# An adaLN block on one core: a new order of the opening steps, and the late modulation weights loaded in quarters

## Chip, cores and metric

The kernel runs on one core of a Trainium2 chip (trn2). The metric is device time in microseconds (us) of one launch. "KB" is 1024 bytes.

## The reference, cut to what matters

The input `x` has 2 x 4096 tokens of width 512. A conditioning vector `c` (2 x 512) gives six modulation rows per batch:

```python
mod = (_silu(L0_c) @ L0_wmod).reshape(2, 6, 1, -1)          # wmod: 512 x (6*512), float32
sa, ca, ga, sb, cb, gb = (mod[:, n] for n in range(6))
ga, gb = signed_floor(ga), signed_floor(gb)                   # magnitude at least 0.25
h = _layernorm(x) * (1 + ca) + sa
x = x + ga * attn(h)      # rms norm with gamma, h @ W_qkva.T (512 -> 3*512), y = scan(sigmoid(a), kv), q*y
h = _layernorm(x) * (1 + cb) + sb
x = x + gb * ffn(h)       # gate, up (512 -> 1408), silu(gate)*up, down (1408 -> 512)
```

All inputs and weights of `ffn` are quantized to a 4-bit grid in blocks of 16 along the contracted axis. `attn` runs along the tokens: `y` at a token is `a` times `y` of the token before plus `kv`. The modulation rows are numbered 0 to 5 here, in the order `sa, ca, ga, sb, cb, gb`.

## The kernel before, in words

The attention half works on 16 blocks of 512 tokens. A block has four tiles of 128 tokens and, for the projections, four groups of 128 output channels. One pair (block, group) is a slot; slots are numbered block after block, four to a block, so slot 4 is the first of the second block. In a slot `mix` (L414 on, the matmul at L430) makes the three projections of one group: 3 parts of 12 matmuls of 128 x 512, in hi and lo halves of float16. Slots 0 to 3 are the opening, written out as one list of words, `OPENING` (L698); slots from 4 on come from the loop at L847.

Every engine executes its instructions in the order in which the program names them (L846, a manual schedule), and so does the sync engine (SP), which issues nearly all DMAs: a word further left in `OPENING`, or a call further up in the loop, is earlier in the queue of its engine. The words that matter here, with a tile number g or with a group e and a piece k behind them:

- Loads, all on SP: `xl_g` a tile of x (L360, 256 KB); `wl e_h` half of a group of W_qkva (L292, 384 KB); `wm s_k` one quarter (128 of 512 rows, 256 KB) of the weights of modulation row s (`load_mod`, L223). `c` and `gT` are small.
- Modulation of the first batch: `ms s_k` multiplies one quarter of wmod with the conditioning vector on TensorE (PE, L230), spread over all partitions; `ca` (L790) and `sa` (L791) copy rows 1 and 0 out of PSUM. `rows` (L244) makes rows 0, 1, 2 for both batches, `rst` and `rdm` copy and send them, `rtr`, `gqa`, `gqf` turn and floor row 2.
- A tile's layer norm: `mo`, `ag` statistics (L154, L159, VectorE = DVE), `rs` (L164, GpSimd = POOL), `ce` (L170) and `sh` (L176) on DVE, `xq` square (L385, ScalarE = ACT), `xg` on POOL (L390, L392), `xh` the hi half on ACT (L398), `xo` the lo half on DVE (L403), and `xt` the DMA transpose of both halves on SP (`norm_turn`, L409).
- A group's weights: `sq` (ACT, L295), `sum` (PE, L300), `cl`, `pw`, `dg`, `sp` (PE, L329), `sc` (DVE, L334), `hi` (ACT, L343), `lo` (DVE, L348).
- `mm e_q`: group 0 of the first block is done in four quarters of 128 tokens, 36 matmuls of 128 x 128 each, so that `mm0_q` needs only the transpose of tile q. For groups 1 to 3, q is one of the three parts, over all 512 tokens.
- After that, `ga`, `sn`, `cy`, `ro`, `yh`, `yt`, `jo`, `re`, `od`: gate, scan, read-out, a second DMA transpose (`yt`, L471), residual, store.

In the loop a slot issues on SP, in this order: two weight tiles of the feed-forward half (256 KB each, only to find their block maxima), a tile of x for seven tiles later (256 KB), the transpose `xT` of the tile four ahead, the transpose `yt`, and last any modulation load. Four `xT` tiles must have landed before the first slot of the next block can begin. There is one `yh` buffer.

The weights of modulation rows 3, 4 and 5, needed only in the feed-forward half, are loaded in the loop. With `MODS = 10` (L844) a whole one (1024 KB) is loaded at the end of slots 5, 6 and 7; the 24 matmuls of `mod_rows(3, 4, 5)` (L244) follow in slot 10, and the rows are stored in slot 11. Slot 5 also loads two rows for the second batch (L283, 256 KB each). The rows 3 and 4 are read back first in slot 36.

```python
            if MODS - 5 <= slot < MODS - 2:
                load_mod(slot - MODS + 8)
```

The feed-forward half then runs over 64 tiles of 128 tokens, 72 matmuls for gate and up (L946) and 33 for down (L993) per tile.

Of the kernel before, what the change touches and what calls it, by code (L numbers as in the profile page):

```python
# [20 lines left out]
KC = D // P  # L21
# [23 lines left out]
def tile_adaln_block(  # L45
# [24 lines left out]
    def ctile(shape, dtype, name, tag=None):  # L70
        return const.tile(shape, dtype, name=name, tag=tag or name)
# [60 lines left out]
    def run(steps):  # L132
        for _ in steps:
            pass
# [53 lines left out]
    def atile(shape, dtype, name, bufs=1):  # L188
        return apool.tile(shape, dtype, name=name, tag=name, bufs=bufs)
# [23 lines left out]
    gT = atile([P, KC], F32, "gT")  # L213
# [9 lines left out]
    def load_mod(s, k0=0, k1=KC):  # L223
        S.dma_start(
            wm[s][:, k0:k1, :],
            wmod[k0 * P : k1 * P, s * D : (s + 1) * D].rearrange("(k p) e -> p k e", p=P),
        )
# [126 lines left out]
    def norm_load(g):  # L354
        i, t = divmod(g, KC)
        if i not in xrows:
            xrows[i] = apool.tile([P, KC, D], F32, name="xr", tag="xr", bufs=4)
        xld[g] = xrows[i][:, t, :]
        b, t0 = divmod(g * P, N)
        S.dma_start(xld[g], x[b, t0 : t0 + P, :])  # L360

    def norm_moments(g):
        xstat[g] = moments(xld[g])
# [51 lines left out]
    def new_xT():  # L415
        return apool.tile([P, 2 * KC, TB], F16, name="xT", tag="xT", bufs=2)
# [4 lines left out]
    def mix(i, xT, e, got):  # L421
        ps = [bank(3 * (e % 2) + j) for j in range(3)]
        got.append((i, e, ps))
        width = P if i == 0 and e == 0 else TB
        for t in range(0, TB, width):
            for pp, part in zip(ps, PARTS):
                n = 0
                for k in range(KC):
                    for wp, xp in PASSES:
                        T.matmul(  # L430
                            pp[:, t : t + width],
                            wqT[e][:, wp, k, part, :],
                            xT[:, xp * KC + k, t : t + width],
                            start=n == 0,
                            stop=n == 3 * KC - 1,
                        )
                        n += 1
                yield

    def gates(i, e, ps):  # L440
        sig = apool.tile([P, TB], F32, name="sig", tag="sig", bufs=1)
        A.activation(sig, ps[0], AF.Sigmoid, scale=us[:, e, 2:3])
        return i, e, ps, sig
# [137 lines left out]
    rows = [(i, col, w, ams) for i in range(IC) for col, w, ams in ((0, w_gate, am_g), (1, w_up, am_u))]  # L581
# [13 lines left out]
    def load_units(items):  # L595
        got = []
        for kind, arg in items:
            if kind in ("max", "rows"):
                got.append((kind, arg, load_rows(arg[2], arg[0])))
            elif kind in ("maxd", "down"):  # L600
                got.append((kind, arg, load_down(*arg)))
            else:
                got.append((kind, arg, None))
        return got
# [84 lines left out]
    ca = [ctile([P, D], F32, "ca0", tag="mod_c0"), None]  # L689
    sa = [ctile([P, D], F32, "sa0", tag="mod_s0"), None]  # L690
# [5 lines left out]


    OPENING = """  # L698
    warm0 wl0_1 gT wl0_0 c xl_0 xl_1 wm1_0 xl_2 sq0_2 wm1_1 sq0_3 wm1_2 xl_3 sq0_1 wm1_3
    sq0_0 wm0_0 mo_0 sg sum0 wm0_1 mu wm0_2 cl0 ag_0 pw0 mo_1 wm0_3 ms1_0 wl1_0 ag_1 dg0  # L700
    wl1_1 rc0 mo_2 xl_7 rs_0 sp0 wm2_0 ag_2 ms1_1 sc0_0 wm2_1 rs_2 wm2_2 sc0_1 ms1_2 wm2_3
    sc0_3 hi0_0 xl_10 rs_1 mo_3 xl_9 ms1_3 wl2_0 sc0_2 xl_4 ag_3 lo0_0 ms0_0 rs_3 ca hi0_1
    ce_2 ms0_1 ce_0 ms0_2 ce_1 ms0_3 warm1 ce_3 sq1_0 lo0_2 sa sq1_1 sh_0 sq1_2 sh_2 xq_0
    sh_1 sq1_3 xg_0 mo_7 xq_1 sum1 sh_3 xh_0 xg_1 cl1 ag_7 xq_2 xo_0 rows pw1 xh_1 ce_7 xt_0
    xg_2 xq_3 rc1 mo_9 xl_6 dg1 xh_2 xo_1 wl2_1 sq2_1 ag_9 xt_1 xo_2 rs_9 sq2_0 sp1 mm0_0
    mo_4 rst2 xg_3 xt_2 rst0 sc1_0 rst1 ag_4 rdm0 sc1_2 wl3_1 xh_3 rtr rs_7 sc1_1 xl_8 xo_3
    mm0_1 gqa rdm1 hi1_0 sc1_3 xt_3 rs_4 sh_7 sq2_2 mo_6 xl_5 xq_7 mm0_2 wl3_0 gqf hi1_1
    xg_7 ag_6 sq2_3 pg_0 rs_6 lo1_2 xh_7 mm0_3 ce_4 lo1_0 sum2 ga_0 pg_1 mm1_0 cl2 sq3_2
    mo_5 pw2 sq3_0 sh_4 sq3_1 dg2 ag_5 xq_4 sn_0 sp2 sq3_3 xg_4 mm1_1 sc2_0 cy_0 sc2_1 rs_5
    xh_4 sc2_2 hi2_0 sc2_3 sum3 ro_0 hi2_1 mm1_2 cl3 lo2_0 yh_0 pw3 lo2_2 dg3 ga_1 yt_0 rc3  # L710
    sn_1 mm2_0 ce_6 cy_1 ro_1 jo_0 sh_6 sp3 mm2_1 yh_1 re_0 sc3_2 sc3_1 xq_6 yt_1 sc3_3 od_0
    sc3_0 hi3_1 xg_6 ce_5 mm2_2 hi3_0 lo3_2 xh_6 lo3_0 xo_4 mm3_0 sh_5 xt_4 pg_3 xq_5 xo_6
    xg_5 rc2 xt_6 xo_7 mm3_1 ga_2 mo_8 xh_5 xt_7 xo_5 sn_2 xt_5 mm3_2 pg_2 cy_2 ag_8 ro_2
    rs_8 ce_8 yh_2 sh_8 yt_2 xq_8 xg_8
    """

    def opening(xT, nxT):
# [118 lines left out]
    def step(gen, n=1):  # L836
        for _ in range(n):
            if gen is not None:
                next(gen, None)

    units, coming = [], []
    rows = None
    NS = NBLK * KC
    MODS = 10  # L844
    plan = [[]] * (KC + 1) + plan
    order = tc.manual_schedule(engines={V.engine, A.engine, G.engine, S.engine, T.engine})  # L846
    with order:  # L847
        xT, nxT = new_xT(), new_xT()
        gate, joining = opening(xT, nxT)
        for slot in range(KC, NS + 3):  # L850
            i, e = divmod(slot, KC)
            if e == 0 and slot < NS:
                xT = nxT
                nxT = new_xT() if i + 1 < NBLK else None
            units, coming = coming, load_units(plan[slot]) if slot < len(plan) else []
            g = slot + KC
            if g + 3 < NT:
                norm_load(g + 3)
            cur = None
            if slot < NS:  # L860
                got = []
                step(mix(i, xT, e, got), 3)
                cur = got[0]
            late = rows
            rows = mod_rows(3, 4, 5) if slot == MODS else None
            if slot == KC:
                gate = gates(*gate)
            if len(joining) == 2 or slot >= NS + 2:
                store(*residual(*joined(*joining.pop(0))))
            if g < NT:  # L870
                norm_hi(g)
            if gate is not None:
                gate = scan(*gate)
                carry_on(*gate)
            if g + 2 < NT:
                norm_moments(g + 2)
            if gate is not None:
                gate = read_out(*gate)
            if g < NT:
                norm_lo(g, nxT)  # L880
            if gate is not None:
                joining.append(turned(*halves(*gate)))
            if g + 2 < NT:
                norm_stats(g + 2)
            for u in units:
                u.advance(1)
            if g + 1 < NT:
                norm_center(g + 1)
            for u in units:
                u.advance(2)  # L890
                u.advance(3)
            if cur is not None:
                cur = gates(*cur)
            if g + 1 < NT:
                norm_shift(g + 1)
                norm_square(g + 1)
            for u in units:
                u.advance(4)
            coming = [Unit(*c_) for c_ in coming]
            for u in coming:  # L900
                u.advance(0)
            if g + 1 < NT:
                norm_gain(g + 1, G)
            for u in units:
                u.advance(5)
                u.advance(6)
            assert all(u.step == 7 for u in units)
            if MODS - 5 <= slot < MODS - 2:
                load_mod(slot - MODS + 8)
            if late is not None:  # L910
                mod_store(*late)
            if slot == KC + 1:
                ca[1] = mod_load(1, 1, "mod_c1")
                sa[1] = mod_load(0, 1, "mod_s1")
            if slot == NS // 2 + KC:
                mods_for(0)
            if slot == NS // 2 + KC + 2:
                gbs[0] = mod_load(5, 0, "mod_gb")
            if slot in (NS - 6, NS - 5):
                for n in range(2):  # L920
                    n += 2 * (slot - NS + 6)
                    x1s[n] = load_x1(n)
            if NS - 5 <= slot < NS - 1:
                n = slot - NS + 5
                xst[n] = stats_x(x1s[n])
                if n in (1, 2):
                    run(quant_x(n - 1, x1s.pop(n - 1), xst.pop(n - 1)))
            gate = cur
# [192 lines left out]
```

## Time and profile before

| | |
|---|---|
| median of 3 runs | 1911.56 us (1910.95 to 1913.81) |
| profiled execution, own time | 1914.65 us |
| its span, first to last instruction | 1912.9 us |
| PE busy | 1895.3 us, 99% |
| DVE, ACT, POOL busy | 84%, 52%, 21% |
| granted TensorE clock, mean | 0.998 of full |

The span is cut into stages as follows, by when the matmuls start: the opening up to 63.2 us, attention from there to 538.8 us, the feed-forward half up to the end. Reading: a row of the windows view gives a stretch, its length, busy time with number of instructions for PE, PEld (weight loads, which overlap PE), DVE, ACT and POOL, then the granted TensorE clock, the mean busy share of the 16 DMA engines (it can pass 1 where transfers overlap), and GB/s. A row of the chain of waits is start, duration, what; "DMA xT<-hl" there is the time from the issue of a transpose to its landing. In the timeline, SPq is the issue of a DMA, and its duration is that of the issue alone.

### The profile page before, as it was taken

What the parts mean: (1) busy time and instruction counts of PE and PEld (TensorE: products, weight loads), DVE (VectorE), ACT (ScalarE), POOL (GpSimd) and SP (SyncE); (2) the same over time, 40 slices, a digit from 0 to 9 for tenths busy, and PEclk for the clock granted to TensorE, in tenths of its full rate; (3) what the DMA queues carried; (4) which work ended last, traced back from release to release, by engine and by line L of the source; (5) the groups of instructions that cost most, each with busy time, mean ns of one, the idle gap of its engine ahead of it and who ended that gap; (6) DMA issues with size and microseconds to landing.
All of it is one profiled execution on the core that took longest, in us unless ns stands there. A gap on an engine that the chain in (4) does not pass through costs nothing.

```text
span 1912.9 us, 25829 instructions
## 1 busy us (share of the span) xinstructions
PE 1895.3 (99%) x9342; PEld 902.5 (47%) x9342; DVE 1601.9 (84%) x2670; ACT 998.2 (52%) x1702; POOL 409.6 (21%) x596
## 2 busy tenths in 40 slices
PE   8999999999999999999999999999999999999998
PEld 5444444444444444444444444444444444444444
DVE  7878899999869988888888888878888888888865
ACT  5555577777755444444444444445444544444432
POOL 5545566666420100100000000000000001000000
PEclk9999999999999999999999999999999999999999
DMA  7787789988733533443344333433344334433433
GB/s 219 208 213 196 170 201 201 213 201 198 152 82 69 88 72 64 79 77 67 64 73 80 70 64 79 80 71 72 64 82 77 64 64 79 80 64 64 68 64 58
DMA packets 469040, 203.26 MB, mean 106 GB/s; under 512 B 426102, under 2 KB 427382, under 8 KB 468912
## 3 DMA queue, kind: packets, MB, share of 16 engines
q1 hardware_dynamic: 454464, 168.09, 41.3%
q0 software_dynamic: 14448, 33.52, 9.0%
q8 instruction: 73, 1.20, 0.3%
q14 instruction: 55, 0.45, 0.1%
HBM read 62.86 MB, written 33.58 MB: 50 GB/s over the span
## 4 chain that ended last, share of the span: by engine, by line
PE 95%; DMA 2%; DVE 2%; issue 0%; ACT 0%; SPq 0%; POOL 0%; DVEq 0%; ACTq 0%
PE mm L946 47%; PE sd L993 24%; PE mm L430 23%; DMA xT<-hl 1%; DMA xr<-in_L_attn_x_dram 1%; DMA yt<-yh 1%; PE sd L230 0%; DVE ld L176 0%; PE sd L244 0%; DVE hl L403 0%; DVE xn L107 0%; DVE hid L966 0%; ACT row L267 0%; DVE hhl L126 0%; DVE amh L148 0%
## 5 line engine op out<-in xcount | busy, mean ns | idle before, releaser
L946 PEld LDWEIGHTS <-x2T 128*128 128x128 f16 x4608 | 450.9, 98 | 469.0 <-issue 0.9
L430 PE MATMUL mm<-xT,wqT 128*128 128x512 f16 (+1 forms) x2412 | 501.0, 370 | 7.0 <-DMA xT<-hl 6.9
L946 PE MATMUL mm<-wuT,x2T 128*128 128x512 f16 (+1 forms) x2304 | 487.7, 361 | 0.6 <-DVE hid L966 0.6
L946 PE MATMUL mm<-wgT,x2T 128*128 128x512 f16 (+1 forms) x2304 | 487.7, 361 | 0.0
L993 PE MATMUL sd<-wdT,hT 128*128 128x512 f16 x2112 | 465.8, 379 | 0.0
L430 PEld LDWEIGHTS <-wqT 128*128 128x128 f16 x2412 | 230.1, 98 | 278.0 <-issue 9.8
L993 PEld LDWEIGHTS <-hT 128*128 128x128 f16 x2112 | 206.7, 98 | 242.7
L961 ACT ACTIVATE silu<-mm,u 128x512 f32<-128x512 f32 (+1 forms) x192 | 124.6, 650 | 285.5 <-PE mm L946 281.8
L966 DVE SCALAR_TENSOR_TENSOR hid<-mm,u,silu 128x512 f32<-128x512 f32 (+1 forms) x192 | 128.5, 673 | 138.4 <-PE mm L946 129.9
L635 POOL TENSOR_SCALAR rstd<-vs 128x1 f32<-128x1 f32 x64 | 14.5, 227 | 989.8 <-ACT sq L633 989.8
L144 ACT ACTIVATE u<-ud,rms 128x1 f32<-128x1 f32 x64 | 18.9, 295 | 278.4 <-DVE rms L140 278.4
L121 ACT ACTIVATE sle<-sl 128x512 f16<-128x512 f32 (+2 forms) x162 | 146.9, 907 | 0.0
L114 ACT ACTIVATE she<-sh 128x1408 bf16<-128x1408 bf16 (+1 forms) x128 | 128.3, 1002 | 4.2
L466 ACT COPY yh<-y 128x1024 uint16<-128x1024 uint16 x64 | 66.9, 1045 | 91.8 <-DVE y L459 76.8
L1017 POOL DMA_DIRECT2D out_dram<-o x63 | 55.5, 881 | 271.0 <-DVE o L1011 267.2
L123 DVE SCALAR_TENSOR_TENSOR xn<-hid,xn 128x1408 f32<-128x1408 f32 x64 | 103.6, 1619 | 3.7 <-ACT hid L117 3.7
L107 DVE TENSOR_TENSOR xn<-hid,inv 128x1408 f32<-128x1408 f32 x64 | 104.0, 1625 | 2.2
L126 DVE SCALAR_TENSOR_TENSOR hhl<-hid,xn 128x1408 f16<-128x1408 f32 x64 | 104.0, 1625 | 2.2
L148 DVE TENSOR_REDUCE amh<-hid 128x88 f32<-128x1408 f32 x64 | 103.7, 1620 | 2.2
L117 ACT ACTIVATE hid<-xn 128x1408 f32<-128x1408 f32 x64 | 88.1, 1377 | 30.9 <-DVE xn L107 30.9
L123 DVE SCALAR_TENSOR_TENSOR xn<-ld,xn 128x512 f32<-128x512 f32 (+1 forms) x98 | 67.0, 684 | 29.0 <-ACT ld L117 28.8
L485 POOL TENSOR_TENSOR xr<-xr,y 128x512 f32<-128x512 f32 x64 | 81.6, 1276 | 19.5 <-ACT y L477 16.0
(129 smaller groups left out, 1913.3 us busy)
## 6 DMA issues: line engine op xcount, KB each, us to landing
ld<-out_dram SPq DMA_DIRECT2D x65, 256.0 KB, 2.9
xr<-in_L_attn_x_dram SPq DMA_DIRECT2D x64, 256.0 KB, 3.5
out_dram<-xr POOLq DMA_DIRECT2D x64, 256.0 KB, 3.9
out_dram<-o POOLq DMA_DIRECT2D x63, 256.0 KB, 3.9
ld<-in_L_ffn_w_gate_dram SPq DMA_DIRECT2D x22, 256.0 KB, 3.2
ld<-in_L_ffn_w_up_dram SPq DMA_DIRECT2D x22, 256.0 KB, 3.3
ld<-in_L_ffn_w_down_dram SPq DMA_DIRECT2D x16, 256.0 KB, 3.3
scratch<-in_L_attn_W_qkva_dram SPq DMA_DIRECT2D x8, 384.0 KB, 5.0
```

Of the source, the lines that this page charges most:

```text
L107: V.tensor_tensor(blocks(xn), blocks(src), spread(inv, nb), ALU.mult)
L114: A.activation(blocks(she), spread(sh, nb), AF.Copy, scale=WPEAK)
L117: A.activation(a, xn, AF.Abs, scale=MAGIC)
L121: A.activation(blocks(sle), spread(sl, nb), AF.Copy, scale=WPEAK)
L123: V.scalar_tensor_tensor(out=xn, in0=a, scalar=FLOOR, in1=xn, op0=ALU.max, op1=ALU.add)
L126: V.scalar_tensor_tensor(out=nq, in0=a, scalar=FLOOR, in1=xn, op0=ALU.max, op1=ALU.subtract)
L148: V.tensor_reduce(am, src.rearrange("p (b k) -> p b k", k=QB), AX.X, ALU.max, apply_absolute_value=True)
L430: T.matmul(pp[:, t : t + width], wqT[e][:, wp, k, part, :], xT[:, xp * KC + k, t : t + width], start=n == 0, stop=n == 3 * KC - 1,)
L946: T.matmul(pp[:, : n1 - n0], x2T[:, xp * KC + k, :], wt[:, wp * KC + k, n0:n1], start=n == 0, stop=n == 3 * KC - 1,)
L961: A.activation(sl[:, :w], pairs[j][0][:, :w], AF.Silu, scale=u[:, 0:1])
L966: V.scalar_tensor_tensor(out=hid[:, n0:n1], in0=pairs[j][1][:, : n1 - n0], scalar=u[:, 1:2], in1=sl[:, : n1 - n0], op0=ALU.mult, op1=ALU.mult,
L993: T.matmul(pd, hT[:, hp * IC + k, :], wdT[:, wd_chunk(wp, k), :], start=n == 0, stop=n == 3 * IC - 1,)
```

## The change

Two things. The word list `OPENING` is a new one: the four transposes of the first block, in the new order 0, 3, 1, 2, are consecutive in SP's queue, where the list before had two loads between the first and the second and two between the third and the fourth. The eleven x tiles, the weight halves and the modulation quarters are the same, in another order; so are the compute words of all engines. And rows 3 to 5 of the modulation weights are loaded in twelve quarters, one at the end of each of the slots 5 to 16, with the matmuls in slot 19 and the stores in slot 20.

SP's queue around the first transposes, by words:

```
before: ... wl1_0 wl1_1 xl_7 wm2_0 wm2_1 wm2_2 wm2_3 xl_10 xl_9 wl2_0 xl_4
        xt_0 xl_6 wl2_1 xt_1 xt_2 wl3_1 xl_8 xt_3 xl_5 wl3_0
after:  ... wl1_1 wl1_0 wm2_3 xl_5 wm2_2 wm2_0 wm2_1 xl_4 wl2_1 wl2_0
        xt_0 xt_3 xt_1 xt_2 xl_10 xl_9 xl_7 xl_6 wl3_1 wl3_0 xl_8
```

The diff, its long lists cut to the parts spoken of:

```diff
-    warm0 wl0_1 gT wl0_0 c xl_0 xl_1 wm1_0 xl_2 sq0_2 wm1_1 sq0_3 wm1_2 xl_3 sq0_1 wm1_3
-    sq0_0 wm0_0 mo_0 sg sum0 wm0_1 mu wm0_2 cl0 ag_0 pw0 mo_1 wm0_3 ms1_0 wl1_0 ag_1 dg0
...
-    sh_1 sq1_3 xg_0 mo_7 xq_1 sum1 sh_3 xh_0 xg_1 cl1 ag_7 xq_2 xo_0 rows pw1 xh_1 ce_7 xt_0
-    xg_2 xq_3 rc1 mo_9 xl_6 dg1 xh_2 xo_1 wl2_1 sq2_1 ag_9 xt_1 xo_2 rs_9 sq2_0 sp1 mm0_0
-    mo_4 rst2 xg_3 xt_2 rst0 sc1_0 rst1 ag_4 rdm0 sc1_2 wl3_1 xh_3 rtr rs_7 sc1_1 xl_8 xo_3
-    mm0_1 gqa rdm1 hi1_0 sc1_3 xt_3 rs_4 sh_7 sq2_2 mo_6 xl_5 xq_7 mm0_2 wl3_0 gqf hi1_1
-    xg_7 ag_6 sq2_3 pg_0 rs_6 lo1_2 xh_7 mm0_3 ce_4 lo1_0 sum2 ga_0 pg_1 mm1_0 cl2 sq3_2
...
+    warm0 wl0_0 gT wl0_1 c xl_3 xl_1 xl_0 wm1_0 sq0_0 xl_2 sq0_1 wm1_1 wm1_2 sg sq0_3 wm0_0
+    mu wm1_3 sq0_2 mo_3 wm0_1 sum0 ag_3 wm0_2 cl0 mo_1 wm0_3 pw0 wl1_1 ag_1 wl1_0 mo_0 dg0
...
+    ca ce_1 ms0_2 ce_2 ms0_3 warm1 ce_0 sq1_2 ce_3 sa sq1_3 sh_0 sq1_1 sh_3 xq_0 sh_1 sq1_0
+    xg_0 mo_5 xq_3 sum1 sh_2 xh_0 xg_3 cl1 ag_5 xq_1 xo_0 rows pw1 xh_3 ce_5 xt_0 xg_1 xq_2
+    mo_4 dg1 rc1 xh_1 xo_3 xg_2 sq2_2 ag_4 xt_3 xo_1 sp1 rst2 rs_5 sc1_0 xh_2 rtr xt_1 sc1_3
+    rs_4 rst1 xo_2 mm0_0 sq2_3 sc1_2 rdm1 xt_2 sq2_0 sh_5 sq2_1 gqa ce_4 xl_10 sum2 rst0
+    xl_9 mm0_1 xq_5 cl2 rdm0 xl_7 sc1_1 xl_6 pw2 gqf hi1_0 wl3_1 wl3_0 xg_5 sh_4 hi1_1 mm0_2
+    xl_8 pg_0 xq_4 dg2 lo1_0 xh_5 xg_4 lo1_2 mm0_3 xh_4 mo_9 rc2 ag_9 mo_7 rs_9 ga_0 mm1_0
...
-    MODS = 10
+    MODS = 19
...
-            if MODS - 5 <= slot < MODS - 2:
-                load_mod(slot - MODS + 8)
+            if MODS - 14 <= slot < MODS - 2:
+                m, k = divmod(slot - MODS + 14, KC)
+                load_mod(3 + m, k, k + 1)
```

More of the change, by code (lines that the diff above doesn't have):

```diff
@@ L698, in tile_adaln_block @@
     OPENING = """
-    warm0 wl0_1 gT wl0_0 c xl_0 xl_1 wm1_0 xl_2 sq0_2 wm1_1 sq0_3 wm1_2 xl_3 sq0_1 wm1_3
-    sq0_0 wm0_0 mo_0 sg sum0 wm0_1 mu wm0_2 cl0 ag_0 pw0 mo_1 wm0_3 ms1_0 wl1_0 ag_1 dg0
-    wl1_1 rc0 mo_2 xl_7 rs_0 sp0 wm2_0 ag_2 ms1_1 sc0_0 wm2_1 rs_2 wm2_2 sc0_1 ms1_2 wm2_3
-    sc0_3 hi0_0 xl_10 rs_1 mo_3 xl_9 ms1_3 wl2_0 sc0_2 xl_4 ag_3 lo0_0 ms0_0 rs_3 ca hi0_1
-    ce_2 ms0_1 ce_0 ms0_2 ce_1 ms0_3 warm1 ce_3 sq1_0 lo0_2 sa sq1_1 sh_0 sq1_2 sh_2 xq_0
-    sh_1 sq1_3 xg_0 mo_7 xq_1 sum1 sh_3 xh_0 xg_1 cl1 ag_7 xq_2 xo_0 rows pw1 xh_1 ce_7 xt_0
@@ L705, in tile_adaln_block @@
-    xg_2 xq_3 rc1 mo_9 xl_6 dg1 xh_2 xo_1 wl2_1 sq2_1 ag_9 xt_1 xo_2 rs_9 sq2_0 sp1 mm0_0
-    mo_4 rst2 xg_3 xt_2 rst0 sc1_0 rst1 ag_4 rdm0 sc1_2 wl3_1 xh_3 rtr rs_7 sc1_1 xl_8 xo_3
-    mm0_1 gqa rdm1 hi1_0 sc1_3 xt_3 rs_4 sh_7 sq2_2 mo_6 xl_5 xq_7 mm0_2 wl3_0 gqf hi1_1
-    xg_7 ag_6 sq2_3 pg_0 rs_6 lo1_2 xh_7 mm0_3 ce_4 lo1_0 sum2 ga_0 pg_1 mm1_0 cl2 sq3_2
-    mo_5 pw2 sq3_0 sh_4 sq3_1 dg2 ag_5 xq_4 sn_0 sp2 sq3_3 xg_4 mm1_1 sc2_0 cy_0 sc2_1 rs_5
-    xh_4 sc2_2 hi2_0 sc2_3 sum3 ro_0 hi2_1 mm1_2 cl3 lo2_0 yh_0 pw3 lo2_2 dg3 ga_1 yt_0 rc3
@@ L711, in tile_adaln_block @@
[L711 to L714, printed above, removed]
+    warm0 wl0_0 gT wl0_1 c xl_3 xl_1 xl_0 wm1_0 sq0_0 xl_2 sq0_1 wm1_1 wm1_2 sg sq0_3 wm0_0
+    mu wm1_3 sq0_2 mo_3 wm0_1 sum0 ag_3 wm0_2 cl0 mo_1 wm0_3 pw0 wl1_1 ag_1 wl1_0 mo_0 dg0
@@ new lines, in tile_adaln_block @@
+    ms1_0 wm2_3 rc0 ag_0 xl_5 rs_3 mo_2 sp0 wm2_2 sc0_2 wm2_0 ms1_1 rs_1 wm2_1 sc0_3 xl_4
+    ms1_2 ag_2 rs_0 hi0_1 sc0_1 wl2_1 wl2_0 sc0_0 ms0_0 rs_2 lo0_2 hi0_0 ms1_3 lo0_0 ms0_1
+    ca ce_1 ms0_2 ce_2 ms0_3 warm1 ce_0 sq1_2 ce_3 sa sq1_3 sh_0 sq1_1 sh_3 xq_0 sh_1 sq1_0
+    xg_0 mo_5 xq_3 sum1 sh_2 xh_0 xg_3 cl1 ag_5 xq_1 xo_0 rows pw1 xh_3 ce_5 xt_0 xg_1 xq_2
+    mo_4 dg1 rc1 xh_1 xo_3 xg_2 sq2_2 ag_4 xt_3 xo_1 sp1 rst2 rs_5 sc1_0 xh_2 rtr xt_1 sc1_3
+    rs_4 rst1 xo_2 mm0_0 sq2_3 sc1_2 rdm1 xt_2 sq2_0 sh_5 sq2_1 gqa ce_4 xl_10 sum2 rst0
@@ new lines, in tile_adaln_block @@
+    xl_9 mm0_1 xq_5 cl2 rdm0 xl_7 sc1_1 xl_6 pw2 gqf hi1_0 wl3_1 wl3_0 xg_5 sh_4 hi1_1 mm0_2
+    xl_8 pg_0 xq_4 dg2 lo1_0 xh_5 xg_4 lo1_2 mm0_3 xh_4 mo_9 rc2 ag_9 mo_7 rs_9 ga_0 mm1_0
+    mo_6 ag_7 ag_6 sn_0 sq3_2 rs_6 sq3_3 rs_7 sq3_0 ce_7 sp2 mm1_1 sq3_1 sc2_0 cy_0 ga_1
+    sc2_1 ro_0 hi2_0 sc2_3 yh_0 sum3 sc2_2 mm1_2 cl3 hi2_1 yt_0 lo2_0 pw3 lo2_2 dg3 pg_1
+    mm2_0 rc3 sn_1 jo_0 ce_6 cy_1 re_0 sh_7 sp3 ga_2 mm2_1 sc3_1 xq_7 od_0 sc3_0 sc3_3 hi3_0
+    xg_7 sc3_2 ro_1 hi3_1 mm2_2 lo3_0 yh_1 lo3_2 xh_7 yt_1 sh_6 mm3_0 xo_5 xq_6 pg_3 xt_5
@@ L715, in tile_adaln_block @@
+    xg_6 xo_4 mo_8 xh_6 xt_4 mm3_1 xo_7 xo_6 xt_7 sn_2 xt_6 mm3_2 pg_2 cy_2 ag_8 ro_2 rs_8
+    ce_8 yh_2 sh_8 yt_2 xq_8 xg_8
     """
```

## The prediction

> **What bounds the kernel now.** I read the page's busy shares first (PE 99%), then the windows view, then the chain of waits, then the timeline around the gaps. PE is the bound nearly everywhere; the time to be won is where it is idle or slowed.
>
> ```profile
> PE 1895.3 (99%) x9342; PEld 902.5 (47%) x9342; DVE 1601.9 (84%) x2670; ACT 998.2 (52%) x1702; POOL 409.6 (21%) x596
> ```
> ```profile
> 20.00:40.00 20.00, 14.65 (x203) 11.06 (x204) 14.95 (x36) 13.52 (x30) 13.31 (x23) 1.00 0.81 186
> 40.00:60.00 20.00, 20.00 (x106) 9.26 (x105) 18.57 (x33) 13.20 (x23) 11.75 (x14) 1.00 0.27 67
> 60.00:80.00 20.00, 19.95 (x93) 8.91 (x92) 15.92 (x26) 12.80 (x23) 12.46 (x18) 1.00 0.75 189
> 80.00:100.00 20.00, 17.56 (x77) 7.64 (x76) 15.86 (x36) 9.27 (x15) 9.23 (x14) 0.95 1.08 310
> ```
>
> PE loses 5.35 us in 20 to 40 and 2.44 us in 80 to 100. The chain of waits says what ended last at both places (start, duration, what):
>
> ```profile
> 28.19 0.73 ACT hl L398
> 28.94 0.75 DVE hl L403
> ...
> 30.48 6.23 DMA xT<-hl
> 36.71 0.04 issue
> 36.75 2.17 PE mm L430 x36
> ...
> 84.76 5.40 DMA yt<-yh
> 90.16 6.70 DMA xT<-hl
> 96.85 0.05 issue
> 96.90 25.17 PE mm L430 x108
> 122.07 3.54 PE sd L244 x24
> 125.61 194.37 PE mm L430 x900
> ```
>
> The reader is to see two late transposes: the fourth of the first block (6.23 us) and the fourth of the third block (6.70 us), whose landing opens slot 8 at 96.90. SP's timeline shows what was queued ahead of the second:
>
> ```profile
> 77.07 0.58 SPq L224 DMA_DIRECT2D scratch<-in_L_wmod_dram  x1
> 77.75 0.95 SPq L283 DMA_DIRECT2D mod<-modd  x2
> ...
> 80.52 3.70 SPq L409 DMA_TRANSPOSE xT<-hl  x1
> 84.76 3.10 SPq L471 DMA_TRANSPOSE yt<-yh  x1
> 87.92 0.57 SPq L224 DMA_DIRECT2D scratch<-in_L_wmod_dram  x1
> ```
>
> Finer windows give the clock after the gap: 0.50 in 98 to 100, 0.66 in 100 to 102, 1.00 from 102.
>
> **What the Trainium skill says.** "DMA: Bandwidth & Descriptors", section "Queues, rings and completion order": one issuing engine's DMAs are consumed in ring order on each DMA engine. The trace agrees: a transpose lands 2.7 to 2.8 us after its issue where the queue is empty (the first of the opening, those at 55 to 61), 4.8 and 6.2 us behind 640 KB of loads, 9.0 us behind slot 5's 2304 KB. Same page, "Issuing engines are not separate DMA queues": all queues share the same 16 engines, so spreading the loads wins nothing but position; the bytes stay. "TensorE: Matmul & The Clock Gate", Part 1: an idle window of about 3.4 us, free-running, halves the clock until a busy window has passed. Here 2.44 us of idleness sufficed for about 3.5 us at half clock; the trace decides.
>
> **The change part by part.** The sums are against the profiled execution: 1914.65 us, span 1912.9 and 1.75 around it. It lies 3.1 us above the median, 1911.56. I apply the difference to the median.
>
> *1. Spread products, start of the opening.* wm1_0 now stands behind one more tile of x, wm1_3 behind one quarter of row 0. A 256 KB load at the 400 to 420 GB/s seen from 9 to 20 us is 0.64 us. PE runs the eight products of 2 matmuls from 8.94 to 17.87, first at half clock (0.50 from 10 to 12, 1.00 from 13), then every 0.43 us. I take 0.55 us of delay: the first `sh` starts at 19.2 for 18.66. Bounds: 0 (the half clock ends at the same instant) and 5.6 (six more products cold, 0.93 us each). The phase of the clock varies in the kernel before as well, so the upper bound is unlikely to be a difference.
>
> *2. The last `xo`.* On ACT, from 20.0, with durations of the timeline: four squares of 0.73, three `xh` of 0.72, one `sq1` 0.56, one `sq2` 0.56, one `rst` 0.60, sum 6.8: the last `xh` could start at 26.8. POOL makes its factor later: with `pw1` 1.05 and `dg1` 1.20 ahead, at 27.05. So ACT ends it at 27.8 (28.91 before, since two `rst` and one `sq2` of that queue now come after it). DVE: five instructions of 0.69 from 19.2, two small ones, then xo_0, ce_5, mo_4, rc1, xo_3, ag_4, xo_1, two `sc1`: free at 28.05; xo_2 0.75 to 28.8. Before: 29.69.
>
> *3. Transposes.* SP issues one in 1.3 us. By these times: 23.8, 26.1, 27.4, 28.85. No load lies among them; xl_4 and the wl2 halves ahead were issued by about 18 and have drained (DMA share 0.42 in 20 to 24). At 2.8 us, 3.2 where two overlap, the last lands at 32.05 instead of 36.71. The seven loads now behind them (2 MB, 5 us) land by about 36; wl3 is needed first by squares after the gate, about 38. Cover: 2 us.
>
> *4. PE.* sp1 at 26.5, `rtr` 1 us, mm0_0 27.85 to 30.0; `sum2` (its four squares done at 30.1) to 30.4; mm0_1 to 32.6, mm0_2 to 34.8, mm0_3 to 37.0. mm1_0 then starts at 37.0 instead of 39.20. The weights of group 1 are ready at about 35.5 (hi, lo after sc1, 0.83 and 0.95 each). Gain **2.2 us**, bounds 0 and 5.3 (all idleness of 20 to 40). Next late could be the second block's transposes: they hang on sp3, 13.1 us of PE work ahead of slot 4 (50.05 to 63.2). New chain from sp3: 0.2 + four sc3 2.2 + ro_1 0.75 + hi wait 0.15 + lo3 1.8 + sh_6 0.74, then xo_5, pg, xo_4, mo_8, xo_7, xo_6 4.0, landing 2.8: 12.6. It fits by 0.5.
>
> *5. Quarters.* Slot 5 loses 768 KB ahead of slot 6's transposes, slots 6 and 7 the same. At the 297 to 319 GB/s of 80 to 88 that is 2.5 us. The x tile issued at 79.94 landed 8.1 us later and DVE's statistics waited 2.58 us for it; that wait goes. So xo for the fourth tile ends near 88.2, its transpose issues near 88.3 and lands 6.7 - 2.5 = 4.2 us later, at 92.5; slot 7 ends at 94.46. Margin 2.0 us, so the 2.44 us of idleness go, and with them the half clock: 108 matmuls took 25.17 us, 108 x 0.2160 (194.37/900) are 23.32, so 1.85. Gain **4.29 us**; bounds 0 (the margin fails) and 4.29.
>
> *6. What quarters add.* Nine more slots issue 256 KB on SP: 0.5 to 0.6 us of issue in a queue that idles for several us each slot, and 0.87 us of transfer at 300 GB/s. Queued behind it are the next weight tiles, the x tile and `xT`. The fourth tile of block 3 was issued at 124.13, took 4.1, landed at 128.2, needed at 125.61 + 7.78 = 133.4: 5.2 us of cover. Cost taken 0; 0.87 us a slot if the cover were gone. `mod_rows` is the same 3.54 us of PE, in slot 19; its rows are wanted first in slot 36. Its stores (ACT, DVE, POOL) meet block maxima in slot 20 as in slot 11. Both gains lie ahead of the DVE-heavy slots; at 320 the chain is back on PE, so they carry through. The 1.1 us gap at 351 starts from loads in slot 36 and stays.
>
> Sum: -2.2 - 4.29 = -6.5. Profiled execution 1908.2; median **1905.1 us**.
>
> **The rivals.** A measurement of this kernel can tell about 0.2% (3.8 us) from no change.
> *Opening gives nothing*: the later modulation or a cold clock on the spread products eats it, or group 1's weights become last. For it: only 0.5 to 1.5 us of slack on DVE and ACT. Against: the 6.23 us landing is gone in any case. 1911.56 - 4.29 = 1907.3.
> *Quarters give little*: the gap was in the profiled execution (3.1 us above median) rather than in the usual one, or a smaller wait takes its place, for `yt` behind the single `yh` buffer (ACT waited 3.94 us there). Against: the bytes are in every execution. 1911.56 - 2.2 = 1909.4.
> *Nothing is moved, both waits return elsewhere*: 1911.6.
> *Slower*: quarters delay the fourth transpose of three blocks, at slots 8, 12 and 16, each with a gap and half clock of 4.29: 12.87 - 4.29 - 2.2 = +6.4, 1917.9. It decides only once a quarter costs more than the 5.2 us of cover, against 0.87 us.
>
> **How the numbers follow.** Both gains 0.62 (own range 1902.5 to 1907), quarters alone 0.13, opening alone 0.14, nothing 0.05, slower 0.06. Faster: the first and most of the second, 0.73; same 0.20; slower 0.07. The low end takes the opening's upper bound (1911.56 - 5.3 - 4.29 = 1902.0); the high end, 1910.0, takes in the opening alone; left out are nothing and slower.
>
> **What would show it.** In the changed profile: first-block transposes landing in about 3 us each; mm1_0 at 37.0; no PE idleness at slot 8 and clock 1.00 there; transposes of slots 5 to 8 landing in 3 to 5 us; the spread products ending near 18.4. I am wrong if PE waits for xT at slot 12 or 16, if the products stay at half clock past 14, or if the second block's first slot waits.

## The result, and the profile after

| | before | after |
|---|---|---|
| median of 12 runs | 1912.89 us (1910.95 to 1916.62) | 1909.96 us (1907.87 to 1911.53) |
| profiled execution, own time | 1914.65 us | 1910.41 us |
| its span | 1912.9 us | 1908.3 us |

The ratio is 0.9983, 95% interval [0.9975, 0.9992]: 2.9 us less (1.5 to 4.8 by the interval) where 6.5 were forecast. The time lies at the slow end of the forecast range (1902.0 to 1910.0). The gain is less than the 3.8 us (0.2%) that the prediction named as the least to be told from no change, though the interval does not contain 1.

Outside the span, a launch of before takes 1.75 us (1914.65 - 1912.9), and one of after 2.1 us (1910.41 - 1908.3; 2.06 to 2.17 in all twelve). So 0.35 us of what the span gains are lost outside it. Why isn't shown: neither part of the change, alone in e1 and e2 below, has this (1.8 us in both, by the median).

The windows view of the kernel after (columns as before), to be held against the four rows of before:

```profile
20.00:40.00 20.00, 17.17 (x217) 12.10 (x218) 17.20 (x39) 16.16 (x35) 16.35 (x28) 1.00 0.65 182
40.00:60.00 20.00, 20.00 (x105) 9.27 (x104) 19.59 (x35) 10.89 (x19) 7.20 (x10) 1.00 0.33 80
60.00:80.00 20.00, 18.90 (x89) 8.39 (x88) 15.30 (x24) 13.66 (x22) 12.86 (x19) 1.00 0.78 188
80.00:100.00 20.00, 20.00 (x94) 9.05 (x93) 17.14 (x38) 10.04 (x18) 8.66 (x14) 1.00 1.11 274
...
120.00:140.00 20.00, 19.41 (x91) 8.62 (x89) 17.63 (x41) 9.94 (x17) 8.66 (x15) 1.00 0.97 236
```

Both forecast gains are there: PE is busy 2.5 us longer in 20 to 40, and 80 to 100 is full at full clock. But 1.10 us are idle in 60 to 80, and 0.59 in 120 to 140, where before had 0.05 and none. PE's timeline names these places (in brackets the idle time ahead, and what ended it); they are the starts of slots 4 and 12:

```profile
61.82 62.32 PE L430 MATMUL mm<-xT,wqT 128*128 128x512 f16 x288 [1.10 <-issue]
124.74 62.33 PE L430 MATMUL mm<-xT,wqT 128*128 128x512 f16 x288 [0.59 <-DMA xT<-hl]
```

SP's timeline of after gives the transposes of the first and of the second block, and the one that opens slot 12; the chain of waits has its landing:

```profile
23.07 6.71 SPq L409 DMA_TRANSPOSE xT<-hl  x4
...
54.91 5.29 SPq L409 DMA_TRANSPOSE xT<-hl  x4
...
118.88 1.29 SPq L409 DMA_TRANSPOSE xT<-hl  x1
```
```profile
118.88 5.81 DMA xT<-hl
124.74 10.32 PE mm L430 x47
```

The first four land in 2.7 to 3.1 us each. The second four issue back to back, one in 1.35 us, so that the last goes out at 58.95 although its tile was ready at 58.08, and it lands at 61.75; PE had run dry at 60.72. The account of these two spans: -2.43 (opening: `sp2` starts at 39.22 instead of 41.65) + 1.05 (slot 4) - 4.13 (slot 8: 2.44 of idle time and, as the repeated profiles below give it, 1.69 of half clock) + 0.59 (slot 12) + 0.43 (slot 40, whose gap grew from 1.12 to 1.55) = -4.49, the difference of the spans being -4.6. The timed runs show only 2.9.

### The profile page after: what moved, and what is told of

Same layout as the page of the kernel before. It is cut to its first block, busy times and chain, and to the rows that moved or that the text cites. A ratio compares the mean times of both kernels' runs of the same rounds, so it can differ in the third digit from the quotient of the medians.

```text
span 1908.3 us, 25838 instructions
## 1 busy us (share of the span) xinstructions
PE 1893.5 (99%) x9342; PEld 901.9 (47%) x9342; DVE 1603.3 (84%) x2670; ACT 999.1 (52%) x1702; POOL 407.7 (21%) x596
## 4 chain that ended last, share of the span: by engine, by line
PE 92%; DVE 4%; DMA 2%; ACT 1%; issue 1%; POOL 0%; SPq 0%; ACTq 0%; DVEq 0%
PE mm L947 47%; PE sd L994 24%; PE mm L430 20%; DVE ld L176 1%; PE sd L230 0%; DMA yt<-yh 0%; DMA xr<-in_L_attn_x_dram 0%; DVE hl L403 0%; DVE ld L170 0%; ACT y L477 0%; DVE y L448 0%; DMA xT<-hl 0%; DMA scratch<-in_L_wmod_dram 0%; DVE scratch L334 0%; DVE y L459 0%
## 5 line engine op out<-in xcount | busy, mean ns | idle before, releaser
L485 POOL TENSOR_TENSOR xr<-xr,y 128x512 f32<-128x512 f32 x64 | 81.9, 1279 | 18.7 <-ACT y L477 14.8
```

## The experiments

The theory to be tested: the gains of opening and quarters are separate; each is partly given back at the next transpose that is late; and the idle time at slot 8 varies from execution to execution, so that the one profile of before overstated it. The rivals: the whole gain is of one of the two parts; or the new gaps come from elsewhere. "Timed" means the median in rounds with the kernel before on the same chip: 1912.76 us for e1 to e4, 1913.44 for e5 to e8.

### One part alone: e1 and e2

e1 has the new opening, with the loads of before:

```diff
-    MODS = 19
+    MODS = 10
...
-            if MODS - 14 <= slot < MODS - 2:
-                m, k = divmod(slot - MODS + 14, KC)
-                load_mod(3 + m, k, k + 1)
+            if MODS - 5 <= slot < MODS - 2:
+                load_mod(slot - MODS + 8)
```

> Only the new opening; modulation weights three to five whole in slots 5 to 7 and their products in slot 10, as before. Theory (two gains, partly given back): the opening's own gain of 2.4 us and its new gap of about 1.1 us ahead of slot 4 both stay, so about 1.4 us below the kernel before in the timed runs, ratio 0.9993, and the gap at slot 8 is still there, about 2.4 us with some half clock behind it; no gap at slot 12. Rival A (the whole gain is the quarters'): no difference from before, ratio 1.0000. Rival B (the quarters gave little, the opening all): -2.9 us, ratio 0.9985.

Measured: 1911.48 us, ratio 0.9994 [0.9986, 1.0002]. That is 1.3 us less, as the theory has it; the interval doesn't exclude that the opening gives nothing, but the profile has its gain, and the gap of 1.28 us at slot 4. At slot 8 the gap was 1.89 us, and no half clock followed.

e2 is the kernel before with the diff's last two parts (quarters, `MODS = 19`) and the old word list.

> Only the quarters, with the opening of before. Theory: the gap at slot 8 with its half clock goes (-4.3 in the profile) and a gap of about 0.6 us ahead of slot 12 comes if its cause is the lost cover of the products that stood there; slot 4 starts without a gap. So -3.3 to -4.3 us in the profile, ratio 0.9979 to 0.9983 in the timed runs. Rival A (all from quarters): -2.9, ratio 0.9985. Rival B (the quarters gave little): at most -0.8 us, ratio 0.9996.

Measured: 1910.45 us, ratio 0.9989 [0.9980, 0.9997], 2.3 us less: short of the 3.3 to 4.3. The interval takes in the expected ratio and that of both rivals, so the profile has to decide: the gap at slot 8 did not go, it shrank to 0.47 us, and slot 12 had 0.47. Neither part holds the whole gain; together they make 3.6 in the timed runs, against 2.9 for after, which of the three alone has the 0.35 us outside the span.

### How much slot 8 costs: two more profiles of before, two of after

> The kernel before, unchanged, for a second profiled execution. Theory (the idle time at slot 8 depends on where fetches of instructions fall among the transposes, so one profile doesn't give its mean): the gap ahead of slot 8 is there, but its size differs from 2.44 us by 0.4 us or more, or there is no half clock behind it; the opening's two gaps on the transposes are 1.3 and 2.0 us again within 0.2. Rival (the first profile stands for all executions): 2.4 us within 0.2, and 1.8 us more for the half clock.

> The kernel before once more, for a third profiled execution; expectations as for the run ahead of it. Over three executions and that of the opening alone the theory wants a mean loss at slot 8 of 2 to 3 us, half clock included, instead of the 4.29 us that the prediction took.

> The kernel after, unchanged, for a second profiled execution. Theory: the gap of slot 4 is the same (1.1 us within 0.1), as it comes from the order of the opening; that of slot 12 differs from 0.59 us by 0.2 us or more, or one comes ahead of slot 8. Rival: both gaps as in the first profile within 0.1 us.

> The kernel after once more, for a third profiled execution; expectations as for the run ahead of it. Over its executions the theory wants a mean loss at slots 8 and 12 together of 0.5 to 1.2 us.

PE's timeline at slot 8, first of before's second profile, then of its third:

```profile
95.38 23.48 PE L430 MATMUL mm<-xT,wqT 128*128 128x512 f16 x108 [2.12 <-DMA xT<-hl]
```
```profile
94.88 25.17 PE L430 MATMUL mm<-xT,wqT 128*128 128x512 f16 x108 [2.16 <-DMA xT<-hl]
```

The same 108 matmuls take 23.48 us after 2.12 us of idle time and 25.17 after 2.16 (and after the 2.44 of the first profile): the half clock, 1.69 us, is there in some executions only. A size 0.4 us away from 2.44 was not seen; the half clock made the difference. All profiles with modulation loads in slots 5 to 7 or 5 to 16 together (e3, e7 and e8 have them elsewhere): the start of `sp2` near the end of the opening, and idle us ahead of a slot ("-" is below 0.15):

| profile | `sp2` starts | slot 4 | slot 8 | half clock behind | slot 12 | slot 40 |
|---|---|---|---|---|---|---|
| before | 41.65 | - | 2.44 | 1.69 | - | 1.12 |
| before, second | 40.42 | - | 2.12 | no | - | 0.92 |
| before, third | 39.90 | - | 2.16 | 1.69 | - | 1.25 |
| e1, opening alone | 38.79 | 1.28 | 1.89 | no | - | 1.60 |
| e2, quarters alone | 41.48 | - | 0.47 | no | 0.47 | 1.76 |
| after | 39.22 | 1.10 | - | no | 0.59 | 1.55 |
| after, second | 40.15 | 0.67 | - | no | 0.21 | 1.47 |
| after, third | 39.59 | 1.13 | 0.32 | no | - | 1.29 |
| e4, fetch shifted | 39.71 | 0.66 | 1.38 | no | - | 1.51 |
| e5, residual later | 39.03 | 0.38 | - | no | - | 1.25 |
| e6, rows spread | 39.32 | 1.11 | - | no | 0.32 | - |

Whole loads in slots 5 to 7 (four profiles): a mean of 2.15 us of idle time and 0.85 of half clock, 3.0 in all. Quarters (the last seven rows): 0.54 us for slots 8 and 12 together. So the quarters are worth about 2.5 us, which agrees with e2's 2.3, and not 4.29. For after alone the mean at the two slots is 0.37, below the 0.5 to 1.2 expected. The second profile of after missed its expectation at slot 4: there the opening itself ran at half clock for a time (0.91 in 20 to 40), so PE came to slot 4 later. It did so behind gaps of 1.14, 1.01 and 0.42 us, which had left the clock whole in the first profile of after (1.14, 1.02 and 0.42). In before's second profile the opening did so too, and its two gaps on transposes were 1.36 and 0.41 us, not 1.3 and 2.0; in the third they were 1.00 and 2.13.

The opening varies as much as slot 8. PE's timeline at `sp2` in before's first and third profile, then in after's first and third:

```profile
41.65 0.33 PE L329 MATMUL sd<-scratch,scratch 128*128 128x384 bf16 x1
39.90 0.33 PE L329 MATMUL sd<-scratch,scratch 128*128 128x384 bf16 x1
```
```profile
39.22 0.33 PE L329 MATMUL sd<-scratch,scratch 128*128 128x384 bf16 x1
39.59 0.33 PE L329 MATMUL sd<-scratch,scratch 128*128 128x384 bf16 x1
```

Over the four profiles with the old list `sp2` starts at 40.86 us on average, over the ten with the new one at 39.56 (e3 has 41.45, e7 39.54, e8 38.80). That is 1.3 us earlier, not 2.43. A mean gap of 0.96 us at slot 4 (in the eight profiles with the end of the list as in after; e3 has 0.67, e7 1.09) takes most of this back, so that slot 4 itself starts about 0.2 us earlier. The timed runs of e1 have 1.3 us, interval -0.4 to 2.7, so what the opening is worth net is not settled. From the first `sh` to `sp2` the new list does gain 2.3 us, but 1.0 us is lost ahead of it: the first `sh` begins at 17.12 to 18.66 us with the old list (mean 17.84) and at 18.26 to 20.13 with the new one (mean 18.84). The spread products ran at half clock for a time in all ten profiles with the new list (clock 0.50 to 0.58 in 10 to 12 us), with the old one only in before's first and in e2; in before's second and third it was 1.00 there. Whether the new order of the loads brings this about isn't shown.

### What delays the transpose at slot 12: e4

`warm_up((56, 30)[n])` becomes `warm_up((56, 50)[n])`: 20 more empty matmuls ahead of the blocks.

> The kernel after with 50 instead of 30 empty matmuls in the second warm-up, which adds 20 instructions to TensorE's stream, so that every later fetch of its instructions falls some 4 us earlier in the work of the blocks or, seen otherwise, 20 instructions earlier in the program. Theory (the 0.59 us ahead of slot 12 need the fetch at 122.7 us on top of the transposes): that gap goes, to 0.1 or less, and the transpose that landed last in 5.8 us takes 3.3; the time of the whole changes by -0.6 to +0.5 us, as other fetches may meet other transposes. Rival (the loads of the slots alone delay the transpose): the gap stays at 0.4 to 0.8 us.

Measured: 1911.65 us, ratio 0.9993 [0.9985, 1.0001]. The gap at slot 12 is gone and the transpose lands in 3.5 us, but slot 8 has a new gap of 1.38 us, and the time is some 1.7 us above after's: more than expected. The DMA view of after from 122 to 124 us, GB/s in 40 slices of 0.05 us and the queues (packets, MB, share of 16 engines):

```profile
GB/s 128 77 31 10 0 0 0 0 0 0 0 0 0 328 0 0 0 0 0 0 0 0 0 0 0 0 0 0 0 0 0 5 5 10 5 10 10 10 10 5
...
q1 hardware_dynamic: 63, 0.02, 91.6%
q8 instruction: 1, 0.02, 2.9%
```

Between 122.2 and 123.5 no packet starts but one of 16 KB, a fetch of instructions; yet the engines are 92% of the two microseconds busy with 63 packets of the transpose. The windows view of e4, in front of its gap at slot 8, shows the rate falling to half from one stretch to the next, with the engines still busy (the last two columns, DMA share and GB/s):

```profile
91.00:93.00 2.00, 2.00 (x10) 0.78 (x8) 2.00 (x4) 1.24 (x3) 0.34 (x2) 1.00 1.87 259
92.00:94.00 2.00, 1.12 (x6) 0.29 (x3) 1.45 (x2) 2.00 (x4) 1.18 (x3) 1.00 1.33 128
```

Such a fetch comes about every 27.5 us in the attention half (q8 has 73 in the whole run); with the 20 added instructions the fetches that after had at 94.5 and 122.7 were at 92.3 and 119.5. The fourth transpose of block 3 landed in 5.7 to 5.8 us in the three profiles where a fetch fell on it (after, its second profile, e6), and in 3.2 to 3.5 in the six where none did (after's third, e3, e4, e5, e7, e8); in e2, where one came towards its end, in 4.8. So a fetch on top of this transpose goes with 2.4 us more. But half a microsecond decides: in e5 and after's third profile the fetch came as long behind the issue (3.7 to 3.8 us) as in the three delayed ones, and the transpose had just landed. And in after the packets stop at 122.2, 0.4 us ahead of the fetch's own packet. Elsewhere the delay is smaller: at slot 8 e4's transpose took 6.6 us with the fetch, those of after's three profiles 5.4 to 5.8 without. Over all fourteen profiles, from 100 us to the end of the attention half and slot against the same slot, the 60 transposes with a fetch in their first 2.7 us land 0.9 us later on average than the 122 without (0.1 to 2.8 by slot). That the gap at slot 12 moves with the fetch is shown by one run, e4; what stalls what inside the DMA engines isn't.

### Whole loads elsewhere: e3

After, with `if 13 <= slot < 16: load_mod(slot - 10)` in place of the quarters.

> The kernel after, with its three modulation weights loaded whole again, at the ends of slots 13, 14 and 15 instead of 5, 6 and 7, in front of the same products in slot 19. Theory (three whole loads in a row are enough to delay the transposes of the block, anywhere): a gap of about 2.4 us with half clock ahead of slot 16, so some 3 to 4 us slower than the kernel after, near 1913, ratio to before about 1.000. Rival (the gap at slot 8 needed the row loads that slot 5 issues beside them): no gap ahead of slot 16, within 0.5 us of the kernel after, ratio 0.9983.

Measured: 1910.64 us, ratio 0.9988 [0.9980, 0.9996]. PE's timeline at slot 16:

```profile
158.12 12.04 PE L430 MATMUL mm<-xT,wqT 128*128 128x512 f16 x55 [1.09 <-DMA xT<-hl]
```

Between the two theories: whole loads make a gap elsewhere too, but half of that at slot 8 and with no half clock. Even this gap need not be all the loads': in this profile a fetch of instructions fell on the transpose that opens slot 16 (issued at 151.89, it took 6.2 us). Slot 5's row loads (512 KB) may explain part of slot 8, which no run tries apart. Slots 8 and 12, now without modulation loads, have no gap.

### The gap at slot 4: e5

In `OPENING`, `re_0 od_0` (GpSimd's first residual addition and its store) move behind `xg_7`:

```diff
-    mm2_0 rc3 sn_1 jo_0 ce_6 cy_1 re_0 sh_7 sp3 ga_2 mm2_1 sc3_1 xq_7 od_0 sc3_0 sc3_3 hi3_0
-    xg_7 sc3_2 ro_1 ...
+    mm2_0 rc3 sn_1 jo_0 ce_6 cy_1 sh_7 sp3 ga_2 mm2_1 sc3_1 xq_7 sc3_0 sc3_3 hi3_0
+    xg_7 re_0 od_0 sc3_2 ro_1 ...
```

> The kernel after with one thing moved in its opening: GpSimd's first residual addition (L485, with its store) stands behind the gain of the last tile of the second block (xg_7) instead of ahead of that tile's shift (sh_7). Theory (the gap of 1.10 us ahead of slot 4 comes from VectorE's sh_7, 1.76 us beside GpSimd's addition and 0.74 us alone, so that sp3 and with it the four transposes start late): sh_7 takes about 0.75 us, the first transpose issues about 1 us earlier (53.9 instead of 54.91), the gap shrinks to 0.0 to 0.3 us, and the time falls by 0.8 to 1.1 us, to about 1909.0. Rival (the four transposes, 1.35 us apart on SP, wait for something else than that chain): the gap stays at 0.7 us or more, the time as after.

The timeline of after, then of e5 (L176 is `sh_7` on DVE, L485 the addition on POOL):

```profile
46.95 1.57 POOL L485 TENSOR_TENSOR xr<-xr,y 128x512 f32<-128x512 f32 x1 [1.61 <-ACT y L477]
47.30 1.76 DVE L176 SCALAR_TENSOR_TENSOR ld<-ld,rstd,sa 128x512 f32<-128x512 f32 x1
```
```profile
47.13 0.74 DVE L176 SCALAR_TENSOR_TENSOR ld<-ld,rstd,sa 128x512 f32<-128x512 f32 x1
49.70 1.27 POOL L485 TENSOR_TENSOR xr<-xr,y 128x512 f32<-128x512 f32 x1
...
54.01 5.29 SPq L409 DMA_TRANSPOSE xT<-hl  x4
```

Apart, 0.74 and 1.27 us; together, 1.76 and 1.57. The four transposes start 0.90 us earlier, and slot 4's gap falls from 1.10 to 0.38 us, a little short of the 0.0 to 0.3 expected. Measured: 1908.95 us, ratio 0.9980 [0.9973, 0.9987], as expected in time; the profile shows the place, since the interval overlaps after's. The Trainium skill, "GPSIMD Engine Reference", section "1. Specifications", lists contention of GpSimd with VectorE instructions that have two inputs from SBUF; `sh` is one, and the trace agrees.

### The gap at slot 40: e6

The three row loads of the second half go one each to the ends of slots 40, 44 and 48, instead of two in slot 36 and one in 38.

> The kernel after with the three row loads of its second half (L283, 256 KB each) one by one at the ends of slots 40, 44 and 48 instead of two at the end of slot 36 and one at the end of slot 38. Theory (these loads delay the turned tiles and through them the transposes of the block that starts at slot 40, where all six profiles so far have a gap of 1.1 to 1.8 us): the gap ahead of slot 40 falls below 0.3 us and none of over 0.3 us comes ahead of slots 44, 48 and 52; time 1.2 to 1.7 us below after, about 1908.5. Rival (the loads of weights that run all through these slots are enough): the gap stays near 1.5 us, the time as after.

Measured: 1908.80 us, ratio 0.9975 [0.9964, 0.9986]. No gap at slot 40, PE busy for all of 300 to 380, none at 44 to 52: as expected. Here too the interval overlaps after's, and the profile shows the place. This gap (0.92 to 1.76 us in the table) was there before the change.

### Quarters later, and all together: e7 and e8

e7 is after with the quarters where fewer other loads are:

```diff
-    MODS = 19
+    MODS = 26
...
-            if MODS - 14 <= slot < MODS - 2:
-                m, k = divmod(slot - MODS + 14, KC)
-                load_mod(3 + m, k, k + 1)
+            for n in range(12):
+                if slot == min(16 + n, 19 + n // 2):
+                    m, k = divmod(n, KC)
+                    load_mod(3 + m, k, k + 1)
```

> The kernel after with its twelve quarters in slots 16 to 24 (one each in 16 to 21, two each in 22 to 24, where no weights are loaded for the planned units) and their products in slot 26. Theory (a quarter in each of slots 5 to 16 still leaves the transposes of slots 7 and 11 with less than 1 us to spare, so that a fetch of instructions that falls on them makes a gap of 0.5 to 1.4 us at slot 8 or 12): no gap of over 0.2 us ahead of slots 8 and 12, nor ahead of 16 to 28, and 0.6 to 1.2 us below after, about 1909.0. Rival (fetch and unit loads make the gaps, the quarters have no part in it): a gap of 0.4 us or more ahead of slot 8 or 12, the time as after.

Measured: 1909.24 us, ratio 0.9979 [0.9973, 0.9986]. No gap at slots 8 and 12; 0.26 us at slot 20, a little over what was expected. Slot 40's gap was 0.13 us there, which the theory didn't foretell: the turned tile that starts it landed in 6.4 us instead of 7.9, with loads unchanged. Why is open; the row loads that e6 moves are not enough to make this gap.

e8 takes e5, e6 and e7 together.

> The three changes of the runs before this together: residual later, row loads spread, quarters later. If each gap is its own: 0.9 + 1.5 + 0.6 = 3.0 us below after, about 1907.0, ratio to before 0.9970. Rival (a gap that is closed gives its time back at the next late transpose): 1908.5 or more.

Measured: 1907.55 us, ratio 0.9971 [0.9960, 0.9982]; the span is 1905.0 us. PE's timeline from slot 4 to the end of the attention half:

```profile
60.68 178.87 PE L430 MATMUL mm<-xT,wqT 128*128 128x512 f16 x828 [0.37 <-issue]
239.47 3.61 PE L244 MATMUL sd<-scratch,sc 128*2 128x512 f32 x24
243.02 287.66 PE L430 MATMUL mm<-xT,wqT 128*128 128x512 f16 x1332
```

No late transpose is left after slot 4, and the span is 3.3 us below after's, as the sum has it (3.0); the timed median is 2.4 below it, 0.35 of which lie outside the span (1.75 us again in e8). Of the kernels tried it has the lowest median, below before's by more than its interval; against after the intervals still overlap.

## Why the prediction was wrong, step by step

The sign, and the mechanism of both gains, were right; their sizes net of what comes next were not. Forecast -6.5; the terms that were off: opening +2.0 (2.2 taken, about 0.2 left at the start of slot 4 on average), slot 8 +1.3 (4.29 taken, 3.0 the mean), new gaps at slots 8 and 12 +0.54, slot 40 +0.34 (mean of three profiles each, 1.44 against 1.10), outside the span +0.35. That leaves -2.0, or -3.1 with e1's timed 1.3 us for the opening, against 2.9 measured, interval 1.5 to 4.8. The account is not good to less than about 1 us.

1. *Spread products*: 0.55 us of delay forecast. Against the first profile of before none shows (first `sh` at 18.68 for 18.66), but that was a late one; over all profiles the delay is 1.0 us (18.84 for 17.84). The step took the half clock to be there in both kernels, and two of the four profiles with the old list had none. The result is inside the bounds, but the term was too small; the rival "opening gives nothing" named this reason.
2. *Last xo*: 28.8 forecast, 28.52 in the chain of after. Right.
3. *Transposes*: four in a row from 23.07, landing in 2.7 to 3.1 us. Right.
4. *PE*: 2.43 us for 2.2 in the first pair of profiles, 1.3 over all. The failed step is its last sentence, that the second block's transposes fit by 0.5. The working added up DVE's instructions at their times alone and let each transpose go when its tile is ready. It left out that SP takes 1.35 us for each of four in a row (0.87 us for the last), and that `sh_7` now falls on GpSimd's addition (1.02 us). e5 takes the second away and gets 0.72 back; the first is read off the timeline, not tried apart.
5. *Quarters*: the gap and the half clock went, but 4.29 us was the loss of one execution, which was itself 1.8 us above the later median; e1 and the repeated profiles give 3.0. The rival "quarters give little" named this reason. The margin of 2.0 us was 0.3: slot 7's transpose landed at 92.7, near the forecast 92.5 (issued 1.0 us earlier, but 5.4 us on its way for 4.2), for a slot that starts at 93.0, not at 94.46: the step left out that the opening's own gain, 1.4 us in this profile, brings PE there sooner. So slot 8 is on an edge, and waits again in three of seven profiles with quarters.
6. *What quarters add*: cost 0 was wrong. The 5.2 us of cover ahead of slot 12 were read off a trace in which `mod_rows` (3.54 us of PE) stood in slot 10; the change moves it behind. What is left is about 2 us (issue 118.88 and 3.2 to land, against 124.15), and with the pause at the fetch the transpose took 5.8. Without `mod_rows` moved this wasn't tried; the numbers of the two traces are the ground. That the gap ahead of slot 40 stays was right.

The prediction named its own end: "I am wrong if PE waits for xT at slot 12 or 16 ... or if the second block's first slot waits". Two of these came. That the median lies next to the 1909.4 us of "quarters give little" is chance: e2 gives the quarters 2.3 us, more than e1 gives the opening. The base was also low by 1.3 us: the median of 3 runs was 1911.56, that of 12 was 1912.89.

## What to carry to other kernels

Before a gap in one profile is given a price, see it in several: its idle time can be stable while what follows it, or the next one, is not. When work is pulled forward, work out the next late wait with the queue's own interval of issue and with who else is busy at that instant, and count as cover only what still stands there after the change. A transfer whose margin is less than a stall that recurs (here 0.9 us on average, 2.4 at slot 12) will sometimes be late.

## What was not expected of the hardware

- A 16 KB fetch of instructions that falls on a DMA transpose goes with a later landing: at slot 12 with 5.7 to 5.8 us instead of 3.2 to 3.5, over the attention half with 0.9 us more on average.
- 2.12 us of idle time on PE left the clock whole, 2.16 halved it for 1.69 us of loss; gaps of 1.14, 1.01 and 0.42 us in the opening did either. The Trainium skill, "TensorE: Matmul & The Clock Gate", Part 1, says that the window which decides is free-running; that such nearly equal gaps end differently agrees with it. The full idle window of about 3.4 us that it asks for was not needed here; the measurement decides.
- DVE's `scalar_tensor_tensor` of 128 x 512 took 2.4 times as long (1.76 for 0.74 us) beside GpSimd's addition.
